# Sharing one SBUF tile between a scan buffer and the FFN input, a nine-step order for MoE gating, and spectral matrices moved into the last layer

## Chip, cores and metric

The kernel runs on one NeuronCore of a Trainium2 chip. A core has five engines with instruction streams of their own: TensorE (PE, with its weight loads PEld), VectorE (DVE), ScalarE (ACT), GpSimd (POOL) and SyncE (SP). SP issues nearly all DMAs of this kernel. The metric is the device time of one execution in microseconds (us); lower is better.

## What is computed

The input is 64 images of 11 × 11 tokens with 128 channels (`NB` = 64, `D` = 121, `C` = 128), in float32. Four layers follow one another. Each has a mixer (called conv here) and an FFN, both with a normalisation ahead of them and a residual sum behind. The mixers are alike, the FFNs are not: a mixture of experts (MoE) in layer 0, a recurrent net in layers 1 and 2, a spectral layer (STU) in layer 3.

```python
# mixer (layers 0..3), cut
xc, z = jnp.split(x @ in_proj_w.T, 2, axis=-1)
xc = silu(conv1d(xc) + conv_b)                 # 256 inner channels, 3 taps, over HW as channels
delta = softplus(dt_proj(x_dbl[:, :, :8]) + dt_proj_b)       # two directions k = 0, 1
dA = jnp.exp(delta[..., None] * A)
dBu = delta[..., None] * Bs * xs[..., None]
h = scan(dA, dBu)                              # h = dA * h + dBu, 16 states
y = einsum(h, Cs) + Ds * xs
out = norm(y) * gelu(z) @ out_proj_w.T

# FFN 0 (MoE, 64 experts, 8 tokens each)
probs = softmax(x @ gate_w.T + gate_b, axis=1)               # over the tokens
vals, idx = top_k(probs.transpose(0, 2, 1), 8)
pooled = einsum(gathered, vals)                # then two expert products, scattered back

# FFN 1, 2 (RNN)
yt = sigmoid(wx_t + yt @ V.T)                  # 121 steps, wx batch-normalised

# FFN 3 (STU): bands i of length 121, 60, 30, 15
out_i = einsum('btkd,k,kde->bte', U_plus, sigma ** 0.25, M_phi_plus[i])
      + einsum('btkd,k,kde->bte', U_minus, sigma ** 0.25, M_phi_minus[i])
      + ar(u, M_u[i])                          # weighted sum over i
```

## The kernel before

**Layers and hand-over.** `metaformer_kernel` runs the layers. Between conv and FFN the activations go through DRAM tiles `mid[0]` to `mid[6]`. Conv of layer l writes `mid[2l]`, chunk by chunk; the FFN loads all of it into `X` (121 partitions × 64 × 128, from a pool `X{l}` opened for the FFN, L1392), adds its result into `X` in place, and stores it into `mid[2l+1]`, which the next conv reads. The helper `mixer` makes the next conv's object, and its `weights` (L99 to L157) issues the loads and builds the small tiles of that conv during the FFN ahead of it (`made` is what is left of that for a later place).

**Conv.** 64 images are worked in 8 chunks (`NC`) of `CB` = 8 images; each chunk has two directions. `Conv.run` writes the order out by hand (a plan of steps, inside `manual_schedule`): what stands in the program is what each engine executes, in order. Per chunk, `lead` loads `x` (L199), takes statistics (L208), normalises, transposes and multiplies (pc, L244); `steps(c, k)` makes delta and its three bf16 parts `d` for the scan: `parts` (relu and abs, L302), `e` (exp, then 1 + exp on ACT, L305 and L307), `ln` (L311), `less` and `delta` on DVE, then `first` (a CAST of the highest part on ACT, L323), `rest` (what remains, POOL, L330), `second` (CAST, L333), `third` (POOL, L336) and `store` to DRAM. `d` has two buffers. From DRAM the parts come back as `R`, are multiplied into `da` (L663), exponentiated (ACT L676), and scanned on DVE (L684). The scan's results alternate between two buffers of 32 KB per partition:

```python
self.H = [fixed.tile([128, 2 * L, 16], F32, name=f"H{i}") for i in range(2)]
self.spare = [x.rearrange("p a w -> p (a w)") for x in self.H]
```

While no scan has begun, `spare` is used as scratch: for the first half chunk (c = 0, k = 0, flag `alone`) the tiles of `steps` lie in `spare[1]` and the bias of the convolution in `spare[0]`. At the end of a conv `last` works in `spare[0]`: `load` brings back `y` (L545), `ahead` and `finish` do the last normalisation, product and residual add (`xo`, L555), and store (L595).

**MoE.** `moe_layer` takes 8 groups of 8 images. In the FFNs the order on each engine is set by a scheduler, which starts from the order of the calls and may move an instruction past others that it does not depend on. Per group: `norm` (the helper `layer_norm`: statistics L52, aggregates L54 on DVE; Ln L56, Exp L57, eight applies L60 on ACT), `front` (transposes, copies, logits), `softmax` (DVE, with Exp on ACT and two operations on POOL, top-8 by max and match_replace) and `back` (transposes of the weights P, copy L936, pooling products L940, copy L941). The loop's order was

```python
xn[g + 1] = norm(g + 1); pr[g] = front(xn[g])
back(g - 2, xn[g - 2]); softmax(g - 1, pr[g - 1])
```

Then the 64 experts run in groups of four, with weights streamed through four buffers.

**RNN.** `rnn_layer` normalises and multiplies 8 groups into `wx`, takes the batch statistics, and runs 121 steps (PE L1186, ACT L1189), each waiting for the last. Then products `px` (L1194) add into `X`. In layer 2, `stu_matrices` runs beside it: a generator whose `next` is called in each step. It loads scaling weights and the filters (`F`, `W`), loads the M matrices of the STU in pieces `m` of 128 × 2048, multiplies `W` (128 × 105) into them (`pa`, L1098), and stores the result `ka` to a DRAM tile `KD` (105 × 16384).

**STU.** `stu_layer` builds `filt`, loads `M` and `MU` (L1248, L1252), then for seven groups of 8 images: `turned_in` (norm, transposes `pt`, L1277) of the next group and `last_band` (filter products `pu` L1287 and accumulating products `acc` L1290, L1292) of this one. The copies out of PSUM alternate between DVE and ACT (`leave`, L1267 and L1269). Behind the groups, the three shorter bands load `K` from `KD` (L1322, three buffers) and multiply (L1329); then the outputs are turned and the last group follows.

Of the kernel before, what the change touches and what calls it, by code (L numbers as in the profile page):

```python
# [16 lines left out]
D = 121  # L17
# [26 lines left out]
def layer_norm(cx, pool, dst, src, eps):  # L44
# [14 lines left out]
    for i in range(G):  # L59
        nc.scalar.activation(  # L60
            dst[:, i, :], src[:, i, :], AF.Identity, bias=r[:, 1, i : i + 1], scale=r[:, 0, i : i + 1]
        )
# [20 lines left out]
class Conv:  # L83
# [75 lines left out]
    def buffers(self, fixed, work, ps_f, dram):  # L159
        nc, NC = self.nc, self.NC  # L160
        self.work = work

        self.H = [fixed.tile([128, 2 * L, 16], F32, name=f"H{i}") for i in range(2)]
# [27 lines left out]
    def lead(self, c):  # L191
# [5 lines left out]
        def begin():  # L197
            s["x"] = work.tile([D, CB, C], F32, name="x", bufs=1)
            nc.sync.dma_start(s["x"], self.src(c * CB, CB))  # L199
            if c == 0:  # L200
                s["bias"] = self.spare[0][:D, :L]
                nc.sync.dma_start(s["bias"], self.cx.a[f"L{self.l}_conv_conv_b"].to_broadcast([D, L]))
            s["st"] = work.tile([D, CB, 6], F32, name="st", bufs=1)
            s["r"] = work.tile([D, 2, CB], F32, name="r", bufs=1)

        def stats(b):
            for i in (b, b + 1):
                nc.vector.bn_stats(s["st"][:, i, :], s["x"][:, i, :])  # L208
# [6 lines left out]
        def scales2():  # L215
            self.rsqrt(s["r"], s["mv"], self.cx.eps6[:D])
# [4 lines left out]
        def normal(b):  # L221
            x, r = s["x"], s["r"]
            for i in (b, b + 1):
                nc.scalar.activation(
                    x[:, i, :], x[:, i, :], AF.Identity, bias=r[:, 1, i : i + 1], scale=r[:, 0, i : i + 1]
                )
# [47 lines left out]
    def steps(self, c, k, start, apart, late):  # L274
# [4 lines left out]
        for b in range(0, CB, 2):  # L279
# [3 lines left out]
            def tile(n, b=b):  # L283
                if alone:
                    at = 1024 * b + 512 * ("relu", "abs", "w", "ln").index(n)
                    return self.spare[1][:, at : at + 512]
# [17 lines left out]
            def e(s=s, tile=tile):  # L304
                nc.scalar.activation(s["p"], s["abs"], AF.Exp, scale=-1.0)  # L305
                s["w"] = tile("w")
                nc.scalar.activation(s["w"], s["p"], AF.Identity, bias=self.one)  # L307
# [21 lines left out]
            def rest(s=s):  # L329
                nc.gpsimd.tensor_sub(s["relu"], s["relu"], s["d"][:, 0, :])  # L330
# [4 lines left out]
            def third(s=s):  # L335
                nc.gpsimd.tensor_sub(s["d"][:, 2, :], s["relu"], s["d"][:, 1, :])  # L336
# [420 lines left out]
    def run(self):  # L757
# [82 lines left out]
        load(1)  # L840
        finish()

# [17 lines left out]
def moe_layer(cx, l, load):  # L860
# [6 lines left out]
    with ExitStack() as ctx:  # L867
# [26 lines left out]
        def norm(g):  # L894
            xn = work.tile([D, GB, C], F32, name="xn", bufs=4)
            layer_norm(cx, work, xn, X[:, GB * g : GB * g + GB, :], cx.eps5)
            return xn

        def front(xn):
            pl = ps.tile([2 * E, HB, D], F32, name="pl", tag="mm")  # L900
            for h in range(2):
                pt = ps.tile([C, HB, D], F32, name="pt", tag="mm")
                for i in range(HB):
                    nc.tensor.transpose(pt[:, i, :], xn[:, HB * h + i, :], ident[:D, :D])
                xT = work.tile([C, HB, D], F32, name="xT")
                nc.scalar.copy(xT, pt)
                nc.tensor.matmul(pl[E * h : E * h + E], gate_wT, xT, start=True, stop=True)
            pr = work.tile([2 * E, HB, D], F32, name="pr", bufs=3)
            nc.scalar.activation(pr, pl, AF.Identity, bias=gate_b)
            return pr  # L910

        def softmax(g, pr):
# [3 lines left out]
            nc.scalar.activation(pr, pr, AF.Exp)  # L916
            tot = work.tile([2 * E, HB], F32, name="tot")
            nc.vector.reduce_sum(tot, pr, axis=AX.X)
            nc.vector.reciprocal(tot, tot)
            nc.gpsimd.tensor_mul(pr, pr, bcast(tot, D))  # L920
            top = work.tile([2 * E, HB, 8], F32, name="top")
            Pg = P[:, g]
# [7 lines left out]
        def back(g, xn):  # L930
            Pg = P[:, g]
            pp = ps.tile([D, HB, 2, E], F32, name="pp", tag="mm")
            for i in range(HB):
                nc.tensor.transpose(pp[:, i].rearrange("p h e -> p (h e)"), Pg[:, i, :], ident)
            PT = work.tile([D, HB, 2, E], F32, name="PT")
            nc.vector.tensor_copy(PT, pp)  # L936
            pq = ps.tile([C, GB, E], F32, name="pq", tag="mm")
            for h in range(2):
                for i in range(HB):
                    nc.tensor.matmul(pq[:, HB * h + i, :], xn[:, HB * h + i, :], PT[:, i, h, :], start=True, stop=True)  # L940
            nc.scalar.copy(pooled[:, :, GB * g : GB * g + GB].rearrange("c e b -> c b e"), pq)  # L941


        xn, pr = {0: norm(0)}, {}
        for g in range(NG + 2):
            if g + 1 < NG:
                xn[g + 1] = norm(g + 1)
            if g < NG:
                pr[g] = front(xn[g])
            if 1 < g:  # L950
                back(g - 2, xn[g - 2])
            if 0 < g <= NG:
                softmax(g - 1, pr[g - 1])
# [91 lines left out]
def stu_matrices(cx, l, keep, work, ps):  # L1045

# [3 lines left out]
    phi, T3, CC, PC = a[p + "phi"], BANDS[3][0], 2048, 256  # L1050
# [23 lines left out]
    W = keep.tile([128, R0[3]], F32, name="W")  # L1074
    for z in range(3):
        nc.vector.tensor_scalar_mul(W[:, R0[z] : R0[z] + NZ[z]], F[:, : NZ[z]], ws[:, z : z + 1])

    def pieces():
        loaded = {}

        def load(c0):
            loaded[c0] = m = work.tile([128, CC], F32, name="m", bufs=3)
            for i in range(4):
                for f0, src in ((0, a[p + "M_phi_plus"]), (16, a[p + "M_phi_minus"])):
                    nc.sync.dma_start(
                        m[32 * i + f0 : 32 * i + f0 + 16], src[i].rearrange("k d e -> k (d e)")[:, c0 : c0 + CC]
                    )

        load(0)
        load(CC)  # L1090
        yield
        for c0 in range(0, C * C, CC):
            if c0 + 2 * CC < C * C:
                load(c0 + 2 * CC)
            ka = work.tile([R0[3], CC], F32, name="ka", bufs=2)
            for j in range(0, CC, PC):
# [362 lines left out]
```

## Time and profile before

| what | us |
|---|---|
| runs of the kernel | 8567.8, 8576.9, 8578.92 (median 8576.9) |
| the profiled execution, its own time | 8578.09 |
| its span in the profile | 8576.3 |
| conv of layer 0, to its last residual add | 0 to 1766.85 |
| MoE gating, first statistics to last pooled copy | 1783.49 to 1887.94 |
| MoE experts, to the last add into X | 1888.0 to 2048.93 |
| conv of layer 1 | 2057.55 to 3814.93 |
| RNN of layer 1 | 3830.42 to 4027.54 |
| conv of layer 2 | 4038.06 to 5794.68 |
| RNN of layer 2, with the M matrices beside it | 5835.52 to 6087.9 |
| conv of layer 3 | 6097.77 to 7852.94 |
| STU | 7878.55 to 8576 |

Mean granted TensorE clock over the span: 0.771.

How to read it: a stage is dated from its first statistics on DVE to its last add. Between the end of one row and the start of the next lies a seam, in which the next stage's data is awaited. In the profile's slices each digit is a fortieth of the span (214 us); a row shows one engine's busy share in tenths, `PEclk` the granted clock of TensorE, `DMA` the busy share of the DMA engines. In a timeline line, `[8.24 <-DMA X<-mid]` says that the engine was idle for 8.24 us before it, and that what ended the idle time was a DMA that writes X.

### The profile page before, as it was taken

What the parts mean: (1) busy time and instruction counts of PE and PEld (TensorE: products, weight loads), DVE (VectorE), ACT (ScalarE), POOL (GpSimd) and SP (SyncE); (2) the same over time, 40 slices, a digit from 0 to 9 for tenths busy, and PEclk for the clock granted to TensorE, in tenths of its full rate; (3) what the DMA queues carried; (4) which work ended last, traced back from release to release, by engine and by line L of the source; (5) the groups of instructions that cost most, each with busy time, mean ns of one, the idle gap of its engine ahead of it and who ended that gap; (6) DMA issues with size and microseconds to landing.
All of it is one profiled execution on the core that took longest, in us unless ns stands there. A gap on an engine that the chain in (4) does not pass through costs nothing.

```text
span 8576.3 us, 209337 instructions
## 1 busy us (share of the span) xinstructions
PE 6028.0 (70%) x83432; PEld 3462.5 (40%) x83432; DVE 6122.9 (71%) x8654; ACT 5803.0 (68%) x12946; POOL 5868.7 (68%) x3171
## 2 busy tenths in 40 slices
PE   5667777666666777666567667766577777766999
PEld 3333334345333444344233334443334444433445
DVE  5888888843888888872788888883388888886211
ACT  6878888732788788762778888863387888885210
POOL 6888888911888888850888888870388888883000
PEclk7777777777787777776677777766677777777999
DMA  6899999945889889960889999972488888896001
GB/s 171 221 222 226 224 223 222 231 121 167 214 224 224 220 222 223 228 175 23 208 219 225 223 223 223 227 197 62 138 219 219 229 225 224 221 230 151 0 4 36
DMA packets 927599, 1605.20 MB, mean 187 GB/s; under 512 B 140075, under 2 KB 612755, under 8 KB 924755
## 3 DMA queue, kind: packets, MB, share of 16 engines
q1 hardware_dynamic: 925339, 1589.70, 74.3%
q8 instruction: 655, 10.73, 0.6%
q14 instruction: 325, 2.66, 0.1%
q10 hardware_dynamic: 1280, 2.10, 0.1%
HBM read 1301.02 MB, written 290.52 MB: 186 GB/s over the span
## 4 chain that ended last, share of the span: by engine, by line
PE 31%; ACT 20%; DMA 18%; DVE 14%; issue 8%; POOL 7%; SPq 2%; DVEq 0%; POOLq 0%; ACTq 0%
DVE H L684 8%; ACT da L676 7%; DMA ub<-uD 5%; POOL ub L652 5%; PE yb L705 4%; PE da L663 4%; DMA ts<-sD 4%; PE pc L244 3%; DMA uD<-u 3%; PE acc L1290 3%; PE out L1329 2%; PE pu L1287 2%; PE pst L1186 2%; PE po L500 2%; DMA R<-dD 2%
## 5 line engine op out<-in xcount | busy, mean ns | idle before, releaser
L652 POOL TENSOR_TENSOR ub<-ub,Bt 128x1024 f32<-128x1024 f32 (+1 forms) x1984 | 4565.9, 2318 | 749.7 <-DMA ub<-uD 545.4
L684 DVE TENSOR_TENSOR_SCAN H<-da,ub 128x512 f32<-128x512 f32 (+1 forms) x3904 | 4495.2, 1197 | 248.8 <-POOL ub L652 120.6
L676 ACT ACTIVATE da<-da,A 128x255 f32<-128x255 f32 x7744 | 3392.4, 447 | 1122.2 <-PE da L663 936.6
L663 PE MATMUL da<-R,pick 120*128 120x255 bf16 x7744 | 1787.7, 325 | 956.2 <-DVE H L684 761.0
L705 PE MATMUL yb<-H,Cz 128*16 128x64 f32 x65536 | 1722.6, 250 | 557.4 <-ACT yst L722 367.7
L705 PEld LDWEIGHTS yb<-H,Cz 128*16 128x16 f32 x65536 | 1165.4, 111 | 1603.6 <-issue 837.7
L663 PEld LDWEIGHTS <-pick 120*128 120x128 bf16 x7744 | 602.4, 105 | 1657.0 <-issue 781.4
L720 DVE TENSOR_TENSOR yst<-yst,yb 128x512 f32<-128x512 f32 (+2 forms) x640 | 340.5, 549 | 277.4 <-PE yb L705 277.3
L170 POOL MEMSET t<- 128x2048 f32 x4 | 7.2, 1805 | 716.2 <-DMA x<-mid 703.1
L244 PE MATMUL pc<-w_conv,xnT 128*121 128x256 f32 x1344 | 445.5, 429 | 56.4 <-ACT t L248 56.4
L722 ACT COPY yst<-yb 128x512 f32<-128x512 f32 (+2 forms) x640 | 330.8, 543 | 112.0 <-DMA yD<-yst 50.0
L295 PE MATMUL pd<-t,w_dt 122*128 122x512 f32 x480 | 355.4, 832 | 57.4 <-ACT t L255 57.4
L327 POOL TENSOR_TENSOR u<-relu,t 128x512 f32<-128x512 f32 x240 | 307.4, 1281 | 22.2 <-DVE relu L318 22.2
L336 POOL TENSOR_TENSOR d<-relu,d 128x512 bf16<-128x512 f32 x240 | 279.0, 1163 | 59.2 <-ACT d L333 59.2
L1267 DVE COPY U<-pu 128x488 f32<-128x488 f32 x128 | 85.3, 666 | 296.6 <-PE pu L1287 277.2
L1269 ACT COPY U<-pu 128x488 f32<-128x488 f32 x128 | 72.9, 570 | 311.8 <-PE pu L1287 304.9
L330 POOL TENSOR_TENSOR relu<-relu,d 128x512 f32<-128x512 f32 x240 | 279.3, 1164 | 6.6
L244 PEld LDWEIGHTS pc<-w_conv,xnT 128*121 128x121 f32 x1344 | 234.7, 209 | 103.4 <-ACT t L248 82.2
L629 POOL TENSOR_TENSOR Cz<-Cp,own 128x512 f32<-128x512 f32 x256 | 274.3, 1071 | 0.0
L361 PE MATMUL pb<-t,x_bc 121*64 121x512 f32 x256 | 174.6, 771 | 132.0 <-ACT bc L366 100.9
L314 DVE SCALAR_TENSOR_TENSOR pd<-w,pd 128x512 f32<-128x512 f32 x240 | 163.8, 683 | 103.2 <-ACT w L307 103.0
L401 PE MATMUL pg<-xnT,in_zT 128*128 128x484 f32 x256 | 156.2, 695 | 110.1 <-ACT g L412 101.2
(238 smaller groups left out, 7509.7 us busy)
## 6 DMA issues: line engine op xcount, KB each, us to landing
ub<-uD SPq DMA_DIRECT2D x1920, 512.0 KB
dD<-d SPq DMA_DIRECT2D x256, 384.0 KB
R<-dD SPq DMA_DIRECT2D x192, 420.0 KB
uD<-u SPq DMA_DIRECT2D x256, 256.0 KB
sD<-s SPq DMA_DIRECT2D x128, 256.0 KB
yD<-yst SPq DMA_DIRECT2D x512, 60.5 KB
ts<-sD SPq DMA_DIRECT2D x56, 512.0 KB
y<-yD SPq DMA_DIRECT2D x112, 242.0 KB
```

Of the source, the lines that this page charges most:

```text
L244: nc.tensor.matmul(pc, lhs, rhs, start=(j == 0), stop=(j == taps - 1))
L295: nc.tensor.matmul(s["p"], self.w_dt[:, k, :], tb[: D + 1], start=True, stop=True)
L327: nc.gpsimd.tensor_mul(s["u"], s["relu"], tb)
L330: nc.gpsimd.tensor_sub(s["relu"], s["relu"], s["d"][:, 0, :])
L336: nc.gpsimd.tensor_sub(s["d"][:, 2, :], s["relu"], s["d"][:, 1, :])
L652: self.nc.gpsimd.tensor_mul(x, x, self.bc[m, "Bt"].unsqueeze(1).to_broadcast([128, n, L]))
L663: self.nc.tensor.matmul(self.da[g % RING][:, j, 1:], self.pick[:n, d % 5].rearrange("p n b -> p (n b)"), self.R[m, d // 35][:n, d % 35 // ...
L676: self.nc.scalar.activation(x, x, AF.Exp, scale=self.A[:, m % 2, d : d + 1])
L684: self.nc.vector.tensor_tensor_scan(self.H[dq % 2][:, :n, p - DQ[dq][0]], self.da[g % RING].rearrange("p j l -> p (j l)")[:, :n], x.rearra ...
L705: self.nc.tensor.matmul(self.yb[32 * q : 32 * q + 16, slot % 8, :, :, :w], self.Cz[slot // 8][:, place % 64 : place % 64 + 2, :].rearrange ...
L720: nc.vector.tensor_add(dst, dst, src)
L722: nc.scalar.copy(dst, src)
```

## The change

It has five parts.

1. A tile `HX` (128 partitions × 32 KB) lives for the whole program. It is the second H of every conv and, on its first 121 partitions, the `X` of every FFN. The pools `X{l}` go. The loads of `X` from `mid` move from the FFN to the end of `Conv.run`: seven chunks behind `load(1)`, the eighth behind `finish`.
2. The first chunk of conv 1 to 3 is read from `X` in SBUF rather than loaded from `mid`. The bias moves to `yst`, the scratch of the first half chunk to `spare[0]`.
3. In the first half chunk (`alone`), 1 + exp, `rest` and `third` go to DVE. `act_tables(nc, 6)` is called in `scales2` of the first chunk.
4. The gating of MoE is cut into nine functions, called in a written-out list with a group offset for each; four groups are under way at once.
5. `stu_matrices` is taken out of the RNN of layer 2. `stu_filters` builds `W` at the start of `stu_layer`, and `matrices(i)` is called behind each of the seven groups: five loads of 128 × 480, products, copies and stores. `M` is one array, concatenated outside the kernel.

```diff
@@ Conv
-        self.H = [fixed.tile([128, 2 * L, 16], F32, name=f"H{i}") for i in range(2)]
+        self.H = [fixed.tile([128, 2 * L, 16], F32, name="H"), cx.HX.rearrange("p (a w) -> p a w", w=16)]
...
-            s["x"] = work.tile([D, CB, C], F32, name="x", bufs=1)
-            nc.sync.dma_start(s["x"], self.src(c * CB, CB))
+            s["x"] = s["in"] = work.tile([D, CB, C], F32, name="x", bufs=1)
+            if c == 0 and self.l > 0:
+                s["in"] = self.cx.X[:, :CB, :]
+            else:
+                nc.sync.dma_start(s["x"], self.src(c * CB, CB))
...
         def scales2():
+            if c == 0:
+                act_tables(nc, 6)
             self.rsqrt(s["r"], s["mv"], self.cx.eps6[:D])
...
-                nc.scalar.activation(s["w"], s["p"], AF.Identity, bias=self.one)
+                if alone:
+                    nc.vector.tensor_scalar_add(s["w"], s["p"], 1.0)
+                else:
+                    nc.scalar.activation(s["w"], s["p"], AF.Identity, bias=self.one)
...
             def rest(s=s):
-                nc.gpsimd.tensor_sub(s["relu"], s["relu"], s["d"][:, 0, :])
+                less = nc.vector if alone else nc.gpsimd
+                less.tensor_sub(s["relu"], s["relu"], s["d"][:, 0, :])
...
             def third(s=s):
-                nc.gpsimd.tensor_sub(s["d"][:, 2, :], s["relu"], s["d"][:, 1, :])
+                less = nc.vector if alone else nc.gpsimd
+                less.tensor_sub(s["d"][:, 2, :], s["relu"], s["d"][:, 1, :])
...
         load(1)
+        X = self.cx.X
+        for c in range(NC - 1):
+            self.nc.sync.dma_start(X[:, CB * c : CB * c + CB, :], self.dst(CB * c, CB))
         finish()
+        self.nc.sync.dma_start(X[:, CB * NC - CB :, :], self.dst(CB * NC - CB, CB))
@@ moe_layer
-        xn, pr = {0: norm(0)}, {}
-        for g in range(NG + 2):
...
+        for g in range(-1, NG + 2):
+            for ahead, f in (
+                (-1, exps),
+                (0, turn),
+                (1, stats),
+                (-1, parts),
+                (-2, turn_p),
+                (0, logits),
+                (-2, pool),
+                (-1, likeliest),
+                (1, lambda g: s[g]["apply"]()),
+            ):
+                if 0 <= g + ahead < NG:
+                    f(g + ahead)
             if g == 1:
                 made()
@@ rnn_layer
-        beside = stu_matrices(cx, l + 1, keep, work, ps) if l == 2 else iter(())
...
-                next(beside, None)
@@ stu_layer
-        sw = scale_weights(cx, l, keep)
+        sw = stu_filters(cx, l, keep)
...
-        for f0, src in ((0, a[p + "M_phi_plus"]), (16, a[p + "M_phi_minus"])):
-            nc.sync.dma_start(M[:, f0 : f0 + 16, :], src[0].rearrange("k d e -> d k e"))
+        nc.sync.dma_start(M, a[p + "M"][:32].rearrange("k (d e) -> d k e", e=C))
...
+        def matrices(i):
+
+            for c0 in range(CC * i, min(CC * i + CC, C * C), CC // 5):
+                cols = slice(c0, min(c0 + CC // 5, C * C))
+                n = cols.stop - c0
+                m = work.tile([128, CC // 5], F32, name="m")
+                nc.sync.dma_start(m[:, :n], a[p + "M"][:, cols])
+                pa = ps.tile([R0[3], CC // 5], F32, name="pa", tag="mm")
+                nc.tensor.matmul(pa[:, :n], cx.W, m[:, :n], start=True, stop=True)
+                ka = work.tile([R0[3], CC // 5], F32, name="ka")
+                leave(ka[:, :n], pa[:, :n])
+                nc.sync.dma_start(cx.KD[:, cols], ka[:, :n])
...
             last_band(b0, u)
+            matrices(b0 // GB)
             u = ahead
@@ metaformer_kernel
+    hold = ctx.enter_context(tc.tile_pool(name="hold", bufs=1))
+    cx.HX = hold.tile([128, NB * C], F32, name="HX")
+    cx.X = cx.HX[:D].rearrange("p (b c) -> p b c", c=C)
...
-        with tc.tile_pool(name=f"X{l}", bufs=1) as pool:
-            cx.X = pool.tile([D, NB, C], F32, name="X")
...
-                made = weights() if l < 3 else None
-                for b0 in range(0, NB, GB):
-                    nc.sync.dma_start(cx.X[:, b0 : b0 + GB, :], mid[2 * l][:, b0 : b0 + GB, :])
-                return made
```

CC is 2400 in the new `stu_layer`, so that seven groups cover the 16384 columns.

## The prediction

> **What bounds the kernel now.** I read the page's slices and chain first, then the timeline at each place that the change touches, then windows of the stages, because the page's means mix four convolution stages with four different FFN stages.
>
> ```profile
> PE   5667777666666777666567667766577777766999
> PEclk7777777777787777776677777766677777777999
> DMA  6899999945889889960889999972488888896001
> PE 31%; ACT 20%; DMA 18%; DVE 14%; issue 8%; POOL 7%; SPq 2%; DVEq 0%; POOLq 0%; ACTq 0%
> ```
>
> The fourth line is the chain's shares: no engine holds it. The long convolution stretches (about 1760 us each) keep the DMA queues at 8 to 9 tenths and the change leaves their steady state alone. It acts on their first 80 us, on the seams between stages, on the gating, and on the last three slices (STU), where PE is the bound at 9 and DMA is empty.
>
> The seams are waits for data that has just been written to DRAM and comes back. Each line of the timeline has start, length, engine, line, operation, and in brackets the idle time before it with what ended it:
>
> ```profile
> 3814.18 0.75 DVE L555 SCALAR_TENSOR_TENSOR xo<-po,norm,xo 121x512 f32<-121x512 f32 x1 [1.34 <-PE po L551]
> 3830.42 1.65 DVE L52 BATCH_NORM_STATS2 ln_st<-X 121x6 f32<-121x128 f32 x8 [1.32 <-DMA X<-mid]
> 4029.34 0.88 SPq L199 DMA_DIRECT2D x<-mid  x1
> 4038.06 1.64 DVE L208 BATCH_NORM_STATS2 st<-x 121x6 f32<-121x128 f32 x8 [9.78 <-DMA x<-mid]
> 5835.52 1.65 DVE L52 BATCH_NORM_STATS2 ln_st<-X 121x6 f32<-121x128 f32 x8 [8.24 <-DMA X<-mid]
> ```
>
> The last residual add of conv 1 ends at 3814.93 and the RNN's first statistics start 15.5 us later; conv 2's last add ends at 5794.68, and there the gap is 40.8 us. Each of these statistics waits for a DMA.
>
> **The change, part by part** (minus is a gain).
>
> *FFN into conv, three times.* The last add into X ends at 2048.93, 4027.54 and 6087.9 and the conv's first statistics follow 8.6, 10.5 and 9.9 us later, behind the DMA that brings back what SBUF held. Reading X directly leaves about 0.6 us of small DVE work each: 29.0 − 1.8 = **−27**. The bias load stays but lands in another tile; its first reader comes later.
>
> *The first half chunk of each conv.* Each d tile needs first, second, third and a store, and the two-buffer d makes CAST number 3 wait for a store:
>
> ```profile
> 56.93 0.62 ACT L323 CAST d<-H 128x512 bf16<-128x512 f32 x1 [4.24 <-DMA dD<-d]
> 63.11 0.62 ACT L323 CAST d<-H 128x512 bf16<-128x512 f32 x1 [4.56 <-DMA dD<-d]
> ```
>
> One such turn is 6.18 us: 2 subtractions on POOL (1.15 + 1.16), 2 CASTs (1.24), and 3.8 of store. On DVE the like subtraction of this shape takes 0.69, so a turn loses 2 × 0.47 = 0.94, over the four serial turns 3.8; the Identity (0.69) that leaves ACT's queue counts where bc copies and exps stand in line, some 1.7 us of the four. DVE is idle there. −5.5 per conv start, ends −3 and −7.5, times four: **−22**. The added table loads would take the automatic ones (2 × 1.28 us) out of the three later starts, −7.7, but in the changed program's order they stand at the program's start and both automatic ones remain at each later start: this part doesn't do what it says. I take 0 here and about +0.5 at most at the beginning, where ACT waits for x until 17.57.
>
> *MoE.* The seam 16.6 falls to 1.5 (small DVE set-up only): −15. Seven chunk loads (3.5 MB, about 17 us at the 200 GB/s of the page) are issued at about 1751, when the second H is free, and only the eighth waits for the last store. Gating:
>
> ```profile
> 1839.87 2.00 PE L940 MATMUL pq<-PT,xn 121*128 121x64 f32 x16
> 1851.42 2.00 PE L940 MATMUL pq<-PT,xn 121*128 121x64 f32 x16 [0.47 <-DVE PT L936]
> 1836.00:1848.00 12.00, 7.90 (x33) 4.29 (x32) 4.60 (x17) 6.17 (x13) 2.30 (x3) 0.78 0.00 0
> ```
>
> The third line is a window: its length, then busy us of PE, PEld, DVE, ACT and POOL, the granted clock, DMA share and GB/s. The period is 11.55 us and no engine is busy for it (PE 7.90 of 12): the order is the limit. Per group ACT has 8 applies 3.17, copies 1.05 + 1.02, pr 0.66, exp 0.61, Ln and Exp 0.51, together 7.0; DVE adds up to 7.0 as well. So the period lies between 7.1 and 11.55. Three engines that hand over to one another within one in-order turn don't reach the floor; I take 8.7. Fill of about 11, seven periods 61 and a tail of 14 from 1768 give the last pooled copy at 1854, for 1887.9: **−33** with the seam (ends −20, −45). The experts behind it are PE-bound, and weights for the first four are in SBUF by about 1825, so it is passed on:
>
> ```profile
> 1945.00:1960.00 15.00, 15.00 (x133) 14.52 (x132) 4.13 (x6) 2.52 (x4) 0.00 (x0) 1.00 0.97 302
> ```
>
> *RNN of layer 1.* The 15.5 us gap does not vanish: PE's order has the next conv's weight products, which need conv_wT, ahead of the first transpose, and that load landed at about 3823.4. The first transpose is held to about 3824, and made()'s two ACT copies (about 2 us) now fall into the ACT-bound loop: **−11** (−8 to −14).
>
> *RNN of layer 2.* From conv end to the first px it takes 279.2 us, the same code in layer 1 198.2. The 81.0 between them is the matrix work beside it: 28 small DMAs and their waits (40.8 against 15.5), Ln and Exp from tables that are reloaded twice a group, the recurrence, and left-over products after the last step:
>
> ```profile
> 5880.63 1.28 ACT L56 ACT_TABLE_LOAD   x1
> 5882.69 1.28 ACT L57 ACT_TABLE_LOAD   x1
> 5887.74 1.28 ACT L56 ACT_TABLE_LOAD   x1
> 6042.65 0.69 PE L1186 MATMUL pst<-ys,VT 128*128 128x64 f32 x2 [0.31 <-ACT ys L1189]
> 6068.68 4.50 PE L1098 MATMUL pa<-m,W 128*105 128x256 f32 x12 [2.17 <-DMA KD<-ka]
> 6073.87 11.44 PE L1194 MATMUL px<-ident,ys 128*121 128x128 f32 x55
> ```
>
> It becomes layer 1 without the matrices: −81 − 11 = **−92** (−85 to −97).
>
> *STU takes them over.* Its start: X no longer comes last behind M and MU, but 20 small loads of the filters stand on SP ahead of M; first acc at conv end + 39 for 51.8: −13 (0 to −20). Then PE does all of this stage:
>
> ```profile
> 7960.00:8010.00 50.00, 50.00 (x129) 23.51 (x128) 10.08 (x16) 14.41 (x27) 0.00 (x0) 1.00 0.00 0
> 8406.20 0.36 SPq L1322 DMA_DIRECT2D K<-KD  x1
> 8411.15 0.56 DVE L1324 TENSOR_TENSOR K<-K,MU 128x384 f32<-128x384 f32 x1 [118.40 <-DMA K<-KD]
> 8445.31 5.24 PE L1329 MATMUL out<-uT,K 128*128 128x510 f32 x6 [2.69 <-issue]
> ```
>
> 34 products of 480 columns at 0.40 (a 488-column acc takes 0.41): +13.8; the copies and stores are under PE. m has two buffers, so the fourth and fifth loads of a group are issued only while its batch is being multiplied, and PE, in order, waits: a load of this size into idle queues took 1.9 us from issue to use (H, 242 KB, 1749.85), the K load 5; I take 3.2 per group, with six or seven groups +20 (0 to +30). The K matrices, loaded at 7878 before, now follow the last KD store: copy 0.6, store 2.6, load and add about 5.7, +9.5, and 2 for PE starting slow after it: +11.
>
> After a stall PE may run slow. The row: a gap of 2.69 us at 8442.6 is followed by six products at 0.87, for 0.42, about 2.5 us lost. [...] by the row 7 × 2.5 = 17. [...] a shorter gap (1.35 us, 8487) shows none; I take +10. STU: −13 + 13.8 + 20 + 11 + 10 = **+42** (+15 to +70).
>
> **Sum**: −27 − 22 − 33 − 11 − 92 + 42 = −143. Against the profiled execution (8578.1 with 1.8 around the span of 8576.3) 8435; the median is 1.2 lower, so 8434.
>
> **The rivals.**
> *(a) STU's turn is dearer:* stalls of 5 us and a slow PE in every group, and K waits longer: STU +80 for +42, 8472. For it: 1 queue of SP carries m, KD and m in order. Against: DMA is idle.
> *(b) The matrices are hidden better:* the loads come in time, STU about +5: 8397. For it: DMA idle at 0 tenths. Against: the two buffers.
> *(c) Order still rules the gating and the first half chunk* (period 11, d's store is the turn): gains of −33 and −22 become −16 and −12: 8461.
> *(d) The table loads do what they are put there for,* −7.7: 8426, inside the range.
> *(e) Slower:* the PE clock. STU has some 600 us of products at clock 1.00. If the waits inside each group (one per 55 us) bring the half rate back and it stays for a share s of the stage, the price is 600 × s (the same work at twice the time). All else sums to −153 (−143 without the +10), so it decides from s = 0.26; s = 0.4 gives 8664. Against it: after 8445 the clock was back within 5.3 us.
>
> **How the numbers follow.** The likeliest 0.50 (8434), (a) 0.17, (b) 0.12, (c) 0.14, (d) 0.03, (e) 0.04. The unknown costs move the likeliest by about ±30 (gating ±13, STU ±28, first half chunk ±8, combined in squares about ±32), which with (a) to (d) makes 8388 to 8486; what is left out is (e) and the outer ends of (a) and (b). About 0.2% (17 us) is what a measurement of this kernel can tell from no change: every case but (e) lies beyond it. Faster 0.95, same 0.02, slower 0.03.
>
> **What would show it.** Right: first statistics within 2 us of the last add at all three conv starts and in MoE; pq 8 to 10 us apart; no table loads in the second RNN's norm loop and px about 188 us after the conv's end; groups of STU growing from 55 to about 60 us with 2 to 4 us of idle PE before the fourth pa; one PE gap of 9 us before the first out. Wrong: pq still 11 us apart; STU groups over 63 us or PE clock below 0.9 there; X's loads ending a wait of ln_st at a seam; the first transposes of the RNN later than 10 us after the conv.

## The result, and the profile after

The changed kernel takes 8459.98 us (median of 8455.56 to 8471.57) where the kernel before takes 8576.88 (8567.8 to 8578.92): ratio 0.9868, 95% interval 0.9851 to 0.9885. A second set of runs, on another occasion, gives 8441.4 for 8542.2: 0.9881 (0.9864 to 0.9898). The profiled execution spans 8458.2 us for 8576.3. The predicted time was 8434, in a range of 8388 to 8486.

The page's slices and the shares of the chain, as for the kernel before:

```profile
PE   5676677676677767767677777666567776766999
PEclk7777777767777777776777777766777778778999
DMA  6888998946898899960899999981689888992111
PE 31%; ACT 20%; DMA 17%; DVE 14%; issue 8%; POOL 7%; SPq 1%; DVEq 0%; POOLq 0%; ACTq 0%
```

The long stretches look alike. What is new is a DMA digit of 1 in each of the last three slices, for 0, 0 and 1: the matrices are loaded and stored there now.

Stage by stage, from the two profiled executions (us):

| piece | before | after | difference | predicted |
|---|---|---|---|---|
| FFN's last add to conv's first statistics, three seams | 29.0 | 2.2 | −26.8 | −27 |
| conv's first statistics to first scan, four times | 277.8 | 268.2 | −9.6 | −22 |
| conv's first scan to last add, four times | 6744.1 | 6713.8 | −30.3 | 0 |
| MoE: conv end to last pooled copy | 121.1 | 97.6 | −23.5 | −33 |
| RNN of layer 1: conv end to px | 198.3 | 188.1 | −10.2 | −11 |
| RNN of layer 2: conv end to px | 279.2 | 191.5 | −87.7 | −92 |
| STU: conv end to first acc | 51.8 | 48.1 | −3.7 | −13 |
| STU: first acc to end | 671.6 | 745.5 | +73.9 | +55 |

The seams, in the timeline of the changed kernel:

```profile
1762.97 0.75 DVE L569 SCALAR_TENSOR_TENSOR xo<-po,norm,xo 121x512 f32<-121x512 f32 x1 [1.42 <-PE po L565]
1768.66 1.64 DVE L52 BATCH_NORM_STATS2 ln_st<-HX 121x6 f32<-121x128 f32 x8 [3.53 <-DMA mid<-xo]
...
5727.60 1.64 DVE L52 BATCH_NORM_STATS2 ln_st<-HX 121x6 f32<-121x128 f32 x8 [6.19 <-DMA mid<-xo]
...
5926.04 0.48 DVE L171 MEMSET yb<- 128x512 f32 x1 [0.25 <-DVE HX L1202]
5926.43 1.58 DVE L215 BATCH_NORM_STATS2 st<-HX 121x6 f32<-121x128 f32 x8
```

The conv's statistics (L215) follow the last add with nothing but a memset between them. The FFN's (L52) still wait, but for a store out of `xo`, not for a load of `HX`: the bracket names `mid<-xo`.

The first half chunk of conv 0, DVE, POOL and ACT lines of the timeline:

```profile
52.57 0.68 DVE L350 TENSOR_TENSOR d<-H,d 128x512 bf16<-128x512 f32 x1
56.22 0.62 ACT L335 CAST d<-H 128x512 bf16<-128x512 f32 x1 [3.72 <-DMA dD<-d]
57.09 1.29 POOL L339 TENSOR_TENSOR u<-H,t 128x512 f32<-128x512 f32 x1 [6.05 <-DMA uD<-u]
57.39 1.53 DVE L350 TENSOR_TENSOR d<-H,d 128x512 bf16<-128x512 f32 x1 [1.48 <-ACT d L346]
61.88 0.62 ACT L335 CAST d<-H 128x512 bf16<-128x512 f32 x1 [4.04 <-DMA dD<-d]
```

CAST to CAST is now 5.66 us for 6.18. `third` (L350) takes 0.68 alone and 1.53 when POOL's `u` (L339) runs at that moment.

The gating, pooling products and a window (length, busy PE, PEld, DVE, ACT, POOL, clock, DMA share, GB/s):

```profile
1824.77 3.68 PE L969 MATMUL pq<-PT,xn 121*128 121x64 f32 x16
1834.59 3.68 PE L969 MATMUL pq<-PT,xn 121*128 121x64 f32 x16
1808.50:1818.30 9.80, 8.84 (x34) 6.14 (x32) 5.57 (x22) 6.28 (x17) 2.21 (x2) 0.50 0.00 0
```

In the first four groups the period is 9.8 to 10.4 us, and the same sixteen products take 3.68 us for 2.00: the clock is at half (0.55 from 1798 to 1808, 0.50 from there to 1838), and at that rate PE is busy for 8.84 of 9.80.

The second RNN, ACT in its norm loop, and then PE:

```profile
5757.31 0.21 ACT L57 ACTIVATE ln_r<-ln_r 121x8 f32<-121x8 f32 x1
5757.43 0.30 ACT L56 ACTIVATE ln_r<-ln_mv,eps 121x8 f32<-121x8 f32 x1
5757.76 3.19 ACT L62 ACTIVATE xn<-HX,ln_r 121x128 f32<-121x128 f32 x8
5911.48 13.58 PE L1200 MATMUL px<-ident,ys 128*121 128x128 f32 x64 [0.31 <-ACT ys L1196]
```

No table load stands between Exp and Ln, and px follows the last step at once.

A group's end in the STU, PE alone, and the start of the products with K:

```profile
7890.95 2.64 PE L1311 MATMUL acc<-uT,MU 128*128 128x488 f32 x6
7893.43 1.77 PE L1295 MATMUL pa<-m,W 128*105 128x480 f32 x4
7897.22 1.02 PE L1295 MATMUL pa<-m,W 128*105 128x480 f32 x2 [2.01 <-DMA m<-in_L_ffn_M_dram]
7899.52 1.90 PE L1295 MATMUL pa<-m,W 128*105 128x480 f32 x2 [1.28 <-DMA m<-in_L_ffn_M_dram]
7901.22 1.82 PE L1283 MATMUL pt<-ident,u 121*128 121x121 f32 x8
7902.83 8.86 PE L1306 MATMUL pu<-filt,u 121*128 121x488 f32 x18
...
8171.49 28.76 PE L1349 MATMUL out<-uT,K 128*128 128x510 f32 x66 [7.36 <-DVE K L1344]
```

Both predicted waits are there, 2.01 and 1.28 us, and the work behind them is slow: `pa` at 0.95 per record, at a clock of 0.50 from 7899.5 to 7903.5. Groups of images are 66.1 us apart on average for 56.4.

### The profile page after: what moved, and what is told of

It is laid out like the page before. It is cut to its first block, busy times and chain, and to the rows that moved or that the text cites. A ratio compares the mean times of both kernels' runs of the same rounds, so it can differ in the third digit from the quotient of the medians.

```text
span 8458.2 us, 209204 instructions
## 1 busy us (share of the span) xinstructions
PE 5994.4 (71%) x83374; PEld 3445.8 (41%) x83374; DVE 6141.0 (73%) x8636; ACT 5768.7 (68%) x12927; POOL 5832.5 (69%) x3139
## 4 chain that ended last, share of the span: by engine, by line
PE 31%; ACT 20%; DMA 17%; DVE 14%; issue 8%; POOL 7%; SPq 1%; DVEq 0%; POOLq 0%; ACTq 0%
ACT da L690 7%; DVE H L698 5%; DMA ub<-uD 5%; POOL ub L666 5%; PE da L677 4%; PE yb L719 4%; PE pc L253 4%; DVE HX L698 3%; DMA ts<-sD 3%; PE pu L1306 3%; PE acc L1309 3%; PE out L1349 2%; DMA uD<-u 2%; PE pst L1193 2%; DMA R<-dD 2%
## 5 line engine op out<-in xcount | busy, mean ns | idle before, releaser
L698 DVE TENSOR_TENSOR_SCAN H<-da,ub 128x512 f32<-128x512 f32 x2048 | 2391.8, 1205 | 93.6 <-POOL ub L666 42.0
L698 DVE TENSOR_TENSOR_SCAN HX<-da,ub 128x512 f32<-128x512 f32 (+1 forms) x1856 | 2115.6, 1187 | 90.5 <-issue 52.4
L719 PE MATMUL yb<-H,Cz 128*16 128x64 f32 x32768 | 867.6, 255 | 349.8 <-ACT yst L736 260.4
L719 PE MATMUL yb<-HX,Cz 128*16 128x64 f32 x32768 | 856.5, 246 | 209.9 <-ACT yst L736 102.5
L719 PEld LDWEIGHTS yb<-H,Cz 128*16 128x16 f32 x32768 | 604.5, 112 | 921.4 <-issue 520.1
L719 PEld LDWEIGHTS yb<-HX,Cz 128*16 128x16 f32 x32768 | 562.4, 110 | 680.7 <-issue 316.8
L339 POOL TENSOR_TENSOR u<-relu,t 128x512 f32<-128x512 f32 x240 | 307.2, 1280 | 22.7 <-DVE relu L330 22.6
L350 POOL TENSOR_TENSOR d<-relu,d 128x512 bf16<-128x512 f32 x240 | 278.6, 1161 | 54.1 <-ACT d L346 53.9
L253 PEld LDWEIGHTS pc<-w_conv,xnT 128*121 128x121 f32 x1344 | 233.7, 209 | 102.8 <-ACT t L257 81.6
```

The source lines that it names most:

```text
L253: nc.tensor.matmul(pc, lhs, rhs, start=(j == 0), stop=(j == taps - 1))
L339: nc.gpsimd.tensor_mul(s["u"], s["relu"], tb)
L350: less.tensor_sub(s["d"][:, 2, :], s["relu"], s["d"][:, 1, :])
L698: self.nc.vector.tensor_tensor_scan(self.H[dq % 2][:, :n, p - DQ[dq][0]], self.da[g % RING].rearrange("p j l -> p (j l)")[:, :n], x.rearra ...
L719: self.nc.tensor.matmul(self.yb[32 * q : 32 * q + 16, slot % 8, :, :, :w], self.Cz[slot // 8][:, place % 64 : place % 64 + 2, :].rearrange ...
```

## The experiments

The theory after the first comparison: the parts act by themselves as predicted at the seams and in the RNNs; the STU is dearer because a product costs two passes and waits bring half clock; the gating is held by the clock; the first half chunk by DVE and POOL. The rival: what the convs lost between first scan and last add (30 us) belongs to the change, and the parts do something else.

The diffs are cut to the lines that matter.

**Each part alone**, put into the kernel before, timed beside it (8544.1 us).

```diff
# hold_only: parts 1 and 2
+        self.H = [fixed.tile([128, 2 * L, 16], F32, name="H"), cx.HX.rearrange("p (a w) -> p a w", w=16)]
+            if c == 0 and self.l > 0:
+                s["in"] = self.cx.X[:, :CB, :]
```

> Parts 1 and 2 of the change alone (one tile for the second H and X, its loads at the end of the conv, first chunk from X). From the stages of the changed kernel: the seams into conv 1 to 3 lose 27 us, those into MoE and the first RNN about 22; the one into the second RNN and into the STU change little, since small loads and M stand ahead there (0 to -20 together). Theory A, that the steady part of the convs (first scan to last add, 30 us shorter in the changed kernel over the four) does not depend on the change and only varies from execution to execution: about -55 us in all and these stretches within 6 us each of before, with no common sign. Theory B, that reading the first chunk from SBUF and the missing DMAs make convs 1 to 3 shorter: -55 - 29 = -84 us, with each of convs 1 to 3 shorter by 5 to 14 us.

Measured: 8458.6 us, ratio 0.9897 (0.988 to 0.9915), about −88 us. The total agrees with theory B, its reason does not. The stages around the convs lost 89 us against the profile of before, which is the whole of it. The convs' stretches summed to 6709.6; that is below the 6744.1 of the profile of before, from another occasion, but not below gate_only and matrices_only, which leave the convs unedited and have 6713.5 and 6684.5. The seams into MoE and the first RNN gave 12.5 and 8, those into the convs 27, and two that I had put at nearly nothing gave the rest: the second RNN 24 net (statistics 31.5 earlier, 8 given back behind them) and the STU 19 (first acc 35.8 us after the conv for 51.8). X no longer stood behind the small loads and the 2 MB of M.

```diff
# gate_only: part 4
+        for g in range(-1, NG + 2):
+            for ahead, f in ((-1, exps), (0, turn), (1, stats), ...):      # nine steps, cut
```

> Part 4 alone, the nine-step order. The changed kernel's pooling products come every 10.0 us for 11.55, with the TensorE clock granted at 0.50 there for 0.72 to 0.85 before. Theory A: the order itself brings this; gating -12 us, period 10.0 and clock 0.5 here too, the rest of the kernel unchanged: about -12 us. Theory B: the half clock comes from what is around (the earlier start, the DMAs of X and of weights at the same time); then the period here is below 9 us with a clock above 0.7 and the gain is -20 us or more.

Measured: 8534.6, ratio 0.9993 (0.9983 to 1.0002): not told from no change. In its profile the gating takes 85.9 us for 104.5, with pooled copies 9.98, 7.92, 8.80 and 8.09 us apart and this clock:

```profile
1823.00:1833.00 10.00, 8.53 (x43) 6.17 (x43) 5.61 (x21) 7.80 (x17) 2.20 (x2) 0.75 0.01 2
```

The interval allows −14 of these 18.6 us. Three kernels that keep the old order (hold_only, alone_only, matrices_only) took 102.8, 101.2 and 98.2 us for the gating in their profiles, so the order is worth 12 to 19. The period is theory B's: the order alone gives the 8.7 us that the prediction took, where the clock is granted at 0.67 to 0.84 (four windows of 10 us). That the half clock comes from what is around, which is theory B's reason, is not shown.

```diff
# alone_only: part 3
+                    nc.vector.tensor_scalar_add(s["w"], s["p"], 1.0)
+                less = nc.vector if alone else nc.gpsimd
```

> Part 3 alone, the first half chunk with 1 + exp, rest and third on DVE. Theory A (the changed kernel's 1.8 to 3.2 us per conv start are all there is, because third takes 1.5 us on DVE whenever POOL multiplies u, for 0.68 otherwise): -2 to -3 us per start, -10 us in all, third at 1.5 us again in two of four turns. Theory B (the prediction's 5.5 per start, of which other parts took some): -22 us.

Measured: 8530.7, ratio 0.998 (0.9972 to 0.9988), −10 to −24 us. First statistics to first scan is shorter by 0.7, 3.6, 2.9 and 4.0 us, 11 in all, with `third` at 1.52 and 1.45 in the second and third turn of the first conv. Nearer to A by its stages; the total doesn't exclude B.

```diff
# matrices_only: part 5
-        beside = stu_matrices(cx, l + 1, keep, work, ps) if l == 2 else iter(())
+            matrices(b0 // GB)
```

> Part 5 alone, the matrices moved from the second RNN into the STU. Theory A, from the changed kernel's stages: second RNN from conv end to px 80 us shorter; STU groups 66 us for 56.4 (seven of them, +68), K wait about +7, the start about as before or later since the small filter loads are added ahead of M and X: together +75 to +85, so -5 to +5 us in all, no gain. Theory B (the prediction's terms): -81 + 52 = about -29 us.

Measured: 8541.0, ratio 0.9993 (0.9984 to 1.0001). Theory A: the second RNN became 80 us shorter, the STU 93 longer. These stages make +13 where the total allows −14 to +1; unedited stages differ too in this profile (the convs sum to 6684.5, the gating takes 98.2 for 104.5). Moving the matrices by itself pays nothing that these runs can tell.

The four differences (−88, −6, −17, −6 of 8544) add up to −117; the whole change's ratios of 0.9868 and 0.9881 are −113 and −102 of it.

**The changed kernel again**, unedited.

> The changed kernel once more, unedited, for the variation of its stages between executions. Theory A (the convs' steady part varies by itself and the half clock in the gating is a matter of phase): the four stretches from first scan to last add sum to anything within 30 us of 6744 and 6714, the gating period is anything between 8.5 and 10.3 us, and the stages outside (seams, RNN, STU) repeat within 2 us. Theory B (both belong to the change): conv stretches again 30 us below those of before on the same chip, pooling products again 10.0 us apart at a clock of 0.50.

Measured: ratio 0.9881. The four conv stretches sum to 6691.4 in this profile, the gating, after two periods of 8.2 and 9.8 us (clock 0.65 from 1798 to 1808), again runs at 0.50 with periods of 9.8 to 10.2, and the STU's group intervals repeat within 0.2 us. The second RNN does not repeat: px comes 198.3 us after the conv for 191.5. The conv stretches differ by 22 us between two executions of one program.

The half clock recurs, but it is not fixed by the program. Two kernels further down, in_place and stu_three, have the same gating code, and in their profiles its first four periods average 8.7 us for 10.1. In in_place three windows have the clocks 0.92, 0.50 and 0.73:

```profile
1798.00:1808.00 10.00, 7.34 (x37) 4.33 (x37) 8.38 (x34) 8.87 (x22) 3.00 (x3) 0.92 0.00 0
1808.00:1818.00 10.00, 9.04 (x35) 6.21 (x32) 5.28 (x18) 5.71 (x13) 1.89 (x3) 0.50 0.01 2
1818.00:1828.00 10.00, 8.52 (x40) 5.58 (x38) 5.40 (x19) 6.50 (x14) 2.73 (x3) 0.73 0.00 0
```

So neither theory holds as it stands: a period of 10 us is common with this order, and not certain.

**Five buffers for m and ka.**

```diff
# stu_deep
-                m = work.tile([128, CC // 5], F32, name="m")
+                m = work.tile([128, CC // 5], F32, name="m", bufs=5)
-                ka = work.tile([R0[3], CC // 5], F32, name="ka")
+                ka = work.tile([R0[3], CC // 5], F32, name="ka", bufs=5)
```

> The changed kernel with five buffers for m and for ka for two, so that a group's five loads are issued ahead and PE never waits for them. Theory A (a product of 480 columns takes two passes, 0.87 us, the two waits 3.3 us a group, and the half clock behind them 2 to 2.5): groups go from 66.1 to about 60.8 us (56.4 + 5 x 0.87), -35 us in all. Theory B (the clock behind the waits comes from something else): the waits alone go, -21 us, groups 62.8 us. Theory C (the products cost the predicted 0.40 and the rest is waiting): groups 58.4 us, -50 us.

Measured: 8404.8, ratio 0.9838 (0.9823 to 0.9853) where the changed kernel beside it has 0.9881: −37 us. Groups are 60.2 us apart. The same place in PE's timeline, and a whole group:

```profile
7863.77 3.38 PE L1295 MATMUL pa<-m,W 128*105 128x480 f32 x8
7866.99 0.99 PE L1283 MATMUL pt<-ident,u 121*128 121x121 f32 x8
7867.82 7.62 PE L1306 MATMUL pu<-filt,u 121*128 121x488 f32 x18
7815.00:7875.00 60.00, 60.00 (x153) 27.63 (x152) 13.49 (x21) 17.16 (x32) 0.00 (x0) 1.00 0.12 38
```

No idle time, clock 1.00; the eight `pt` records take 0.99 us for 1.82, the eighteen `pu` 7.62 for 8.86. Theory A: 5.9 us per group were 3.3 of waits and 2.6 of half clock.

**Three buffers**, one profile.

```diff
# stu_three
+                m = work.tile([128, CC // 5], F32, name="m", bufs=3)
+                ka = work.tile([R0[3], CC // 5], F32, name="ka", bufs=3)
```

> The changed kernel with three buffers for m and ka: a group's first three loads are there ahead, the fourth is issued behind the first product, and only the fifth can be late. Theory A [...]: one wait of 1 to 2 us, products behind it at full rate, groups 61.5 to 62.5 us. Theory B (any wait of over 1 us halves the clock): the same wait, then 3 us or so at half rate, groups 63 to 64.5 us.

```profile
7841.61 2.58 PE L1295 MATMUL pa<-m,W 128*105 128x480 f32 x6
7845.39 1.02 PE L1295 MATMUL pa<-m,W 128*105 128x480 f32 x2 [1.20 <-DMA m<-in_L_ffn_M_dram]
7846.25 0.99 PE L1283 MATMUL pt<-ident,u 121*128 121x121 f32 x8
```

A wait of 1.20 us, and `pt` behind it takes 0.99 us, as with five buffers at a clock of 1.00; groups 61.7 us, 1.5 more than with five buffers. As in theory A, this one short wait costs about its own length, where the two of the changed kernel cost their length and the clock. That the number of waits decides is not shown by it.

**The last add written into X.**

```diff
# in_place
-            nc.vector.scalar_tensor_tensor(xo[q], po[q], self.norm[:, j : j + 1], xo[q], ALU.mult, ALU.add)
+            dst = kept_x(q) if z else xo[q]      # kept_x: the images' place in X, stored from there
+            nc.vector.scalar_tensor_tensor(dst, po[q], self.norm[:, j : j + 1], xo[q], ALU.mult, ALU.add)
-        self.nc.sync.dma_start(X[:, CB * NC - CB :, :], self.dst(CB * NC - CB, CB))
```

> The changed kernel with the last residual add of each conv written straight into X in SBUF and stored from there; the eighth chunk is not loaded back. Theory A (the first statistics at a seam wait for the last store to mid, since their tile lies on the memory of the tile that is being stored): the seams of 4.9, 3.5, 7.6 and 4.4 us fall to 1.5 us in MoE and STU (-3 each) and to about 1.5 before both RNNs, where the transposes then wait for conv_wT, which is loaded earlier by the removed wait on the queue: -2 to -5 each; together -10 to -16 us. Theory B (the statistics really wait for the loads of X, 3.5 MB behind one another): seams unchanged, 0 to -3 us.

Measured: ratio 0.9867 (0.9851 to 0.9884) for 0.9881, within each other's intervals. The statistics start 0.1 to 0.4 us after the last add at all four seams, so the wait was for the store out of `xo`. MoE kept that gain; counted to px, the first RNN kept nothing of 3.3 us and the second 0.8 of 7.5; counted to the first acc, the STU kept nothing. What takes it back in the RNNs no run shows. In the STU it is the small loads on the queue (an SPq line's length is from the first to the last issue of its group, waits included):

```profile
7628.03 1.63 DVE L52 BATCH_NORM_STATS2 ln_st<-HX 121x6 f32<-121x128 f32 x8
7644.82 11.82 SPq L1244 DMA_DIRECT2D sigma<-in_L_ffn_sigma_dram  x1
7663.04 3.58 PE L1241 MATMUL pf<-ahead,turned 121*121 121x488 f32 x4 [36.22 <-DMA sgn<-in_sgn_dram]
```

PE's first product comes 35 us after the statistics, when sigma and sgn have got through behind 22 filter loads.

**Useless products in the gating.** Twelve products per group are added that nobody reads.

```diff
# gate_warm
+        def busy(lhsT, n):
+            for i in range(n):
+                nc.tensor.matmul(fill[: lhsT.shape[1]], lhsT, ident[:k], start=True, stop=True)
...
+                busy(s[g]["xT"][h][:, 0, :], 3)      # behind the logits of each half
+            busy(s[g]["PT"][:, 3].rearrange("p h e -> p (h e)"), 6)      # behind the pooling
```

> The changed kernel with twelve extra products of 128 columns per gating group (six behind the logits, six behind the pooling), whose result nobody reads: about 2.6 us of PE per group at full clock, 5.2 at half. Theory A (the gating is held by PE running at half clock, because it is not busy without a break): the clock rises towards 1.0 and the period falls to 8.5 to 9 us although PE has more to do, -5 to -10 us. Theory B (clock stays at 0.50): period 10.0 + 5.2 = 15 us, +35 us.

```profile
1805.47 1.90 PE L978 MATMUL pq<-PT,xn 121*128 121x64 f32 x16
1814.00 1.90 PE L978 MATMUL pq<-PT,xn 121*128 121x64 f32 x16
1822.00 1.90 PE L978 MATMUL pq<-PT,xn 121*128 121x64 f32 x16
1808.00:1818.00 10.00, 9.77 (x72) 7.73 (x72) 5.26 (x18) 8.32 (x20) 2.21 (x2) 1.00 0.00 0
```

Theory A: the clock goes to 1.00 and the period to 8.0 to 8.5 us, with more for PE to do. The gating takes 85.0 us for 92.6, and the experts 150.2 for 160.5. In the six other profiles with the gating of the changed kernel the gating takes 87.0 to 92.8 and the experts 157.5 to 160.4, so the gain of the experts is clear, that of the gating between 2 and 8. The kernel `together` below repeats the times (periods 8.0 to 8.5 us, experts 149.9). The total is 0.9874 for 0.9881, too near to call.

**u on DVE** in the first half chunk.

```diff
# alone_u
-                nc.gpsimd.tensor_mul(s["u"], s["relu"], tb)
+                (nc.vector if alone else nc.gpsimd).tensor_mul(s["u"], s["relu"], tb)
```

> The changed kernel with u of the first half chunk on DVE too. Theory A (DVE's third takes 1.5 us for 0.68 because POOL's multiplication runs at the same time): every third at 0.7 us, but DVE has 0.69 per u more, so the turn stays at 5.5 to 5.8 us and the start gains 0 to 1 us. Theory B (the 1.5 us have another cause, such as the CAST that still writes d): third stays at 1.5 us in two of four turns and each start loses 1 to 2 us. In all within 5 us of the changed kernel.

```profile
58.17 0.69 DVE L339 TENSOR_TENSOR u<-H,t 128x512 f32<-128x512 f32 x1 [2.97 <-DMA uD<-u]
60.10 0.68 DVE L350 TENSOR_TENSOR d<-H,d 128x512 bf16<-128x512 f32 x1
```

Theory A for the cause: every `third` of the first conv takes 0.68 or 0.69. The turn gains nothing, because `u` waits for its own store and DVE, in order, stands behind it. First statistics to first scan sums to 271.1 us, 268.2 and 270.1 in the two profiles of the changed kernel; ratio 0.9888 (0.9874 to 0.9901).

**STU in six groups of pieces, filters built in the second RNN**, and **all of it together**.

```diff
# stu_early
-    CC = 2400
+    CC = 2880      # six pieces of 480, six buffers each for m and ka
+        if l == 2:      # in rnn_layer, behind the steps
+            nc.vector.tensor_copy(cx.sw, stu_filters(cx, l + 1, keep))
-        sw = stu_filters(cx, l, keep)
+        sw = cx.sw
```

> The changed kernel with six buffers for m and ka, the matrices in six groups of six pieces rather than seven of five, and stu_filters called in the second RNN behind its steps (its loads then fall into the recurrence, where the queue is idle). Against the changed kernel: groups 61.6 us for six and 56.4 for the seventh, so no waits and no half clock (-35 us as with five buffers); the gap of 7.4 us ahead of the first product with K goes, and the slow start behind it (-9); the first acc 24 us after the conv's end for 48, since 20 small loads no longer stand ahead of sigma, M and MU (-20 if M, 2.1 MB, is then not the wait; -10 if it is). Theory A, all three: -54 to -64 us, ratio to before about 0.981. Theory B (K and the start are held by other things): -35 us.

> stu_early, in_place and gate_warm in one kernel. By their stages: -54 to -64 (STU), -10 to -16 (seams; the one into the STU counts once), -5 to -12 (gating and the first experts at full clock): -70 to -85 us against the changed kernel, ratio to before about 0.979. If the seams' gains are given back behind the first statistics, as in the RNNs and the STU of in_place, nearer to -65.

stu_early: 8426.0 for 8573.0, ratio 0.9829 (0.9815 to 0.9842). The K gap went (PE passes from the last acc to K's products without a break), but the start only fell to 42.7 us for 48 to 50, and the second RNN's first step came 70.9 us after the conv for 58.1 and 63.7: the scheduler put the filters' small work into its norm loop, not behind the steps, and DVE stood 6.1 us there for the load of sg. Against the changed kernel's ratios that is −33 to −45 us, theory B's total; by its stages the STU lost 55, and the second RNN took 7 to 14 of it back.

together (with in_place and gate_warm): 8389.0, ratio 0.9788 (0.9774 to 0.9801), below both kernels; its STU's first acc comes 30.3 us after the conv, its gating and experts take 19 us less than the changed kernel's. Against the changed kernel's 0.9868 and 0.9881 that is −68 to −80 us.

## Why the prediction was right, and where its sum was not

The median lies 26 us above the predicted time. Parts of two rivals happened: (a), a dearer STU (+70 where it had +80), and (c), smaller gains in the gating and the first half chunk (−24 and −10 where it had −16 and −12). Of the signs that it named, the statistics came within 2 us of the last add at all three conv starts (0.6 to 1.0), but not in MoE (4.9). One sign of being wrong came too: STU groups over 63 us (66.1), though PE's clock over that stage stayed at 0.97.

- **FFN into conv, −27; first RNN, −11; second RNN, −92:** −26.8, −10.2 and −87.7. The difference between the two RNNs was a sound measure of what the matrices cost there: in matrices_only the second takes 199.1 us, the first 197.7. The first pair of profiles is a favourable one, though: over the six profiles with this RNN code the first RNN takes 188.1 to 194.5 us and the second 191.5 to 198.3, so that the gains lie between −4 and −10 and between −81 and −88. The step by which −11 was reached is only half confirmed: the first transpose of the first RNN came 8.9 us after the conv, as forecast, but in in_place it came after 3.8 and px no sooner.
- **Seam into MoE, −15:** −11.7. The step "only the eighth waits for the last store" failed: the first statistics did as well. What they wait for is a store that reads `xo`, whose memory their tile seems to reuse; in_place, which stores from X, takes the wait away.
- **Gating period 8.7:** right for the order (8.7 on average in gate_only), too small in the changed kernel (10.1 on average over four periods). The term lacked the clock: I read PE's 7.90 of 12 us as slack, and at half rate it is none (8.84 of 9.80 at 0.50). It is a matter of the execution too: with the same gating code in_place and stu_three have 8.7.
- **First half chunk, −5.5 per start:** about −2.4. A turn gained 0.52 us, not 0.94, since `third` on DVE meets POOL's `u`. Of the 1.7 us from ACT's queue 0.3 appeared: from the first relu to the first CAST it is 7.42 us for 7.74. The table loads are off the path as said; the two automatic ones remain at each later start.
- **STU, +42:** +70. The step "34 products of 480 columns at 0.40 (a 488-column acc takes 0.41)" failed by a factor of two, since 0.41 is a record, not a product. The tile view of `pa` in the kernel before shows it:

```profile
L1098 PE MATMUL pa<-m,W x128: 379/379/706, 5897.1 to 6073.7; 128*105 128x256 f32 x128
L1099 DVE COPY ka<-pa x64: 359/424/426, 5899.7 to 6074.1; 105x256 f32<-105x256 f32 x64
```

  Two records per copied product. From stu_deep, a group's five products cost 3.8 us; over all 34 that is 26 us, not 13.8. Waits were 3.3 per group as predicted (22 in all). The half clock cost 2.6 per group (16, for the 10 taken). K's gap of 7.4 and the slow start behind it are 9 (for 11). The start gained 3.7, not 13: its 22 small loads hold sigma and sgn, and hold_only, where these loads stay in the second RNN, gained 16 there.
- **The slow PE behind a wait, +10:** 16. The row (a gap of 2.69 us, and six products at 0.87 for 0.42 behind it, at a clock of 0.50) made it 17; the 10 that was taken was the author's estimate, and the row was the better guide. Waits of 2.01 and 1.28 us with a product between them brought half rate (`pt` at 1.82 us), and 1.20 alone in stu_three did not (0.99). In the gating the breaks are short: in the first profile of the changed kernel PE was busy for 26.9 of the 30 us from 1808 to 1838, with no break over 0.98 us, and its clock stayed at 0.50. What decides, in either place, no run here shows.
- **What covered the misses, and luck:** the terms above make −88 us of stages, 55 short of the sum of −143. By themselves they would have given about 8489, just past the upper end of the range. The convs' stretches, for which the prediction had 0, add −30 in this pair of profiles, and with them the median lies inside. That the number fits so well is in part luck: the profile before has the longest convs of all fourteen profiles (6744.1 us; the others 6684.5 to 6725.0, those with unedited convs among them), and one program differs by 22 us from itself. Whether some of the 30 belongs to the whole change stays open, since both of its ratios (−113 and −102 us) are more than the −88.

## What to carry to other kernels

Count the records of a float32 product, against the copies that take its results (128 for 64 in `pa` here), before a line's mean is used as its price. What an engine left idle at one clock was not slack at another here: TensorE was busy for 7.90 of 12.00 us at 0.78, and in the tighter order for 8.84 of 9.80 at 0.50, which made it the bound. Giving the loads ahead of it more buffers paid here (−37 us); filling TensorE's breaks with useless products raised the clock (1.00 for 0.50) and shortened the experts (150.2 us for 160.5), though the total could not tell. When data no longer has to be loaded, look at what else shares the memory and the queue: here the wait moved to a store, and then to small loads.

## What the hardware showed

- TensorE's clock stayed at 0.50 from 1808 to 1838 us in both profiles of the changed kernel, while PE was busy for 26.9 and 27.5 of these 30 us; in the first of them a break of 0.78 to 0.98 us recurs in every group. With twelve useless products per group (1.56, 0.92 and 0.92 us of records in gate_warm) it was 1.00 from 1798 to 1838.
- A DVE subtraction of 0.68 us took 1.48 to 1.68 when a POOL multiplication of 1.29 us had begun before it: 57.39 to 58.92 us, POOL ending at 58.38. In all eight such cases of the changed kernel's first profile DVE ended 0.54 to 0.56 us after POOL. In the eight without that it took 0.68 or 0.69.
- A store of 242 KB issued at 5720.22, on a queue that had issued seven loads of 484 KB from 5704.10 on, let its waiter go at 5727.60, 7.4 us later.
